# Two ways to bring modulated rows back by token, and a later landing time for gathers

## The chip, the cores and the metric

The kernel is one program on one NeuronCore of a Trainium2 chip. Its metric is the device time of the whole program, in microseconds (us). The engines that work side by side are TensorE (PE in the profile, with its weight loads as PEld), VectorE (DVE), ScalarE (ACT), GpSimd (POOL) and SyncE (SP, which here only issues DMA transfers). Each engine takes its own instructions strictly in the order in which the program lists them, and engines meet by semaphores. Operands lie in SBUF (the on-chip memory of 128 partitions), matmul results in PSUM.

## The reference

There are two layers on `x` of shape 4 batches x 1024 tokens x 256 features, all in float32. Each layer has an attention-like part and a mixture of 8 experts, and before each part a layer norm is modulated with rows that depend on the batch alone:

```python
mod = (_silu(L0_c) @ L0_wmod).reshape(L0_c.shape[0], 6, 1, -1)
sa, ca, ga, sb, cb, gb = (mod[:, 0], mod[:, 1], mod[:, 2], ...)
h = _layernorm(x, axis=-1) * (1 + ca) + sa
x = x + ga * _L0_attn_ref(h, L0_attn_queries, L0_attn_combiners)
h = _layernorm(x, axis=-1) * (1 + cb) + sb
x = x + gb * _L0_ffn_ref(h, L0_ffn_W1, L0_ffn_b1, L0_ffn_W2, L0_ffn_b2, L0_ffn_Wr, L0_ffn_br)
```

The first attention is linear: per head it needs the Gram matrix of the modulated rows `h` over the tokens of a batch, some small products with the query and combiner weights, and one product of `h` with the result. The first expert layer takes the two best of 8 experts for every token. The second layer has the same frame, with a chunked gated MLP for attention and plain matrices as experts.

## The kernel before, in words

**Tiles and stages.** A chunk is 128 tokens of one batch; there are 4 batches `b` of 8 chunks. A "half" is four chunks of a batch, named by a key `(1, b, g)` before the attention and `(2, b, g)` before the experts, so there are 16 halves. The first stage (from 0 to 112.48 us of the span, where the first expert matmul `p_h` L1597 starts) does the attention of layer 0 and the routing. The expert stage and the second layer follow.

**What a half goes through.** `normalised` takes statistics on DVE (L1094, L1095, then L1098 adds the epsilon to the variance), a square root on ACT (L1102), a reciprocal with a Newton step on DVE (L1106 to L1113), and the scaling on ACT (`xn<-x_sb`, L1120). `to_features` turns the 128x128 squares on PE (`pm_t`, L1160), and ACT modulates them while it copies them out of PSUM, with `(1 + c)` and the shift as one number per partition (L1165, to `h1T` or `h2T`). `to_tokens` turns the modulated squares back: 8 turns on PE (`pm_b`, L1187) and two ACT copies (L1192) write the modulated rows over `xn`.

**What needs which form.** For `(1, b, g)` the rows by token feed the Gram matrix (`pm_gram`, L1246, 16 products of a batch, each of which is two records in the profile), whose diagonal blocks DVE copies to `gd` (L1256). Then come a product with the combiners on PE (L1278), an ACT copy (L1288), a product with the queries (`pm_m`, L1299) and the gated copy to `md` on DVE (L1311). `first_half` ends there. `second_half` multiplies the rows by feature with `md` (`pm_o`, L1339), adds to `x_sb` on DVE (L1349), normalises again, turns by `to_features`, computes the router's logits (`pm_e` L194, `le` L1382, `pm_l` L1391), lets DVE choose experts (`route`, 12 operations from L420 to L446) and stores the rows by token, `xn` of `(2, b, g)`, in the DRAM table `h_rows`. The expert stage starts with an indirect DMA by POOL that fetches the rows of the first expert's block from that table (L353), so it waits for the last store.

**What sets the order.** `Plan` is a list scheduler that runs when the program is built. Each piece has an engine, an assumed duration, pieces that it follows, buffer slots, a `rank` (the smaller goes first), an earliest time `at`, and a `lag`: a time after its end at which its result is assumed to be there. `Plan.run` goes through assumed time and puts each piece on its engine's list; the lists are fixed from then on. `FIRSTS` and `SECONDS` are the ranks of the batches' `first_half` and `second_half`. On SP the lists hold the loads and stores, in order: after the gate rows (`gates0`, written to DRAM and read back spread over all partitions as `ga0`), `first_weights` loads W1 and W2 of the last expert into both buffers of each, `w1buf[0]`, `w1buf[1]`, `w2buf[0]` and `w2buf[1]`, then `load_wm1` the second layer's modulation weights, and later the stores to `h_rows`. `kept_busy` puts filler matmuls (`pm_busy`, L1033) into assumed gaps of PE. POOL has nothing to do between its set-up and its first gather.

In the second layer `combine` gathers expert results `yg2` with one POOL DMA each, planned with a `lag` of 1.5 us.

Of the kernel before, what the change touches and what calls it, by code (L numbers as in the profile page):

```python
# [19 lines left out]
P = 128  # L20
B, S, D = 4, 1024, 256
NC = S // P
KD = D // P
E = 8
# [3 lines left out]
EPS = 1e-5  # L28
# [7 lines left out]
FIRST = 8  # L36
ROUTER = 64
STRIP = 32
AHEAD = 3
QUAD = 4  # L40
SQ = 32
# [104 lines left out]
def adaln_d2_kernel(  # L146
# [20 lines left out]
    nc = tc.nc  # L167
# [3 lines left out]
    dram = ctx.enter_context(tc.tile_pool(name="dram", bufs=1, space=DRAM))  # L171
# [48 lines left out]
    def load_mod(wmod, queue, between=()):  # L220
# [8 lines left out]
            )  # L229
        return w  # L230

    busy16 = pa.tile([P, 4 * P], F16, name="busy16", bufs=1)
    nc.vector.memset(busy16, 1.0)
    nc.vector.memset(wr_sb, 0.0)
# [130 lines left out]
    class Pairs:  # L365
# [42 lines left out]
        def route(self, scratch, logits, at, k, step=1):  # L408

            cut = slice(at, at + (k - 1) * step + 1, step)  # L410
            one = self.one[:, :, cut, :]
            shape = [P, k, E]

            def t(tag):
                return scratch.tile(shape, F32, tag=f"r{k}_{tag}", name=f"r_{tag}", bufs=2)

            left = logits
            for i in range(2):
                m = self.best[:, i, cut]
                nc.vector.tensor_reduce(m, left, AX.X, ALU.max)  # L420
                hit = t("hit")
                nc.vector.tensor_tensor(
                    hit, left, m.unsqueeze(2).to_broadcast(shape), ALU.is_equal
                )

                nc.vector.tensor_tensor(
                    hit, hit, rank.unsqueeze(1).to_broadcast(shape), ALU.mult
                )
# [7 lines left out]
                nc.vector.tensor_tensor(  # L436
                    one[:, i, :, :], hit, first.unsqueeze(2).to_broadcast(shape), ALU.is_equal
                )
# [7 lines left out]
            nc.vector.tensor_tensor(both, one[:, 0, :, :], one[:, 1, :, :], ALU.add)  # L446

        def turn(self, pool, h):

# [543 lines left out]


    modT = const.tile([P, 4, B, KD], F32, name="modT")
    gates0 = dram.tile([B, 2, D], F32, name="gates0")
    SA, CA, SB, CB = range(4)
    gds, mds = [
        [pa.tile([P, KD, P], F32, name=f"{x}{i}", bufs=1) for i in range(2)]
# [22 lines left out]
    gate_rows = pa.tile([B, 2, D], F32, name="gate_rows", bufs=1)  # L1022

    stores = []
    plan = Plan(p1=3, p2=2, pm=3, xn1=5, h1T=2, xn2=6, h2T=2, t1=1, le=2)
# [44 lines left out]
    def gate_row(i, column, at):  # L1070
# [12 lines left out]
            rank=-0.5,  # L1083
        )

    def normalised(b, cs, key, slot, after, rank, at=0.0):

        n = len(cs)

        def stats(c):  # L1090
            if c == cs[0]:
                tiles["mv", key] = pa.tile([P, n, 2], F32, tag="ln_mv", name="ln_mv", bufs=6)
            st = pa.tile([P, 6], F32, tag="ln_st", name="ln_st", bufs=4)
            nc.vector.bn_stats(st, x_sb[:, c, b, :])  # L1094
            nc.vector.bn_aggr(tiles["mv", key][:, c - cs[0], :], st)  # L1095
            if c == cs[-1]:
                v = tiles["v", key] = pa.tile([P, n], F32, tag="ln_v", name="ln_v", bufs=6)
                nc.vector.tensor_scalar(v, tiles["mv", key][:, :, 1], EPS, None, ALU.add)  # L1098

        def root():  # L1100
            y = tiles["y", key] = pa.tile([P, n], F32, tag="ln_y", name="ln_y", bufs=6)
            nc.scalar.activation(y, tiles["v", key], AF.Sqrt)  # L1102

        def newton():
            mv, v, y = tiles["mv", key], tiles["v", key], tiles["y", key]
            nc.vector.reciprocal(y, y)  # L1106

            t = pa.tile([P, n], F32, tag="ln_t", name="ln_t")
            nc.vector.scalar_tensor_tensor(t, y, -0.5, y, ALU.mult, ALU.mult)
            nc.vector.tensor_tensor(t, t, v, ALU.mult)  # L1110
            nc.vector.scalar_tensor_tensor(y, t, 1.5, y, ALU.add, ALU.mult)
            m = tiles["m", key] = pa.tile([P, n], F32, tag="ln_m", name="ln_m", bufs=6)
            nc.vector.scalar_tensor_tensor(m, mv[:, :, 0], -1.0, y, ALU.mult, ALU.mult)  # L1113

        def scaled(i):
            if i == 0:
                tiles["xn", key] = pa.tile(
                    [P, n, D], F32, tag=slot[0], name=slot[0], bufs=plan.room[slot[0]]
                )
            nc.scalar.activation(  # L1120
                tiles["xn", key][:, i, :],
                x_sb[:, cs[i], b, :],
                AF.Identity,
                bias=tiles["m", key][:, i : i + 1],
                scale=tiles["y", key][:, i : i + 1],
            )

        last = []
        for i, c in enumerate(cs):
            last = [  # L1130
                plan(
                    DVE,
                    0.54 if i < n - 1 else 0.71,
                    lambda c=c: stats(c),
                    after=[*last, *after(c)],
                    rank=rank,
                    at=at,
                )
            ]
# [37 lines left out]
    def to_tokens(key, slot, src, held, after, rank):  # L1177
# [17 lines left out]
            done.append(plan(ACT, 0.6, out_, after=[m], holds=[ps, slot], rank=rank))  # L1195
        return done

    def buffer(key, tag, shape):


        def get():
            if key not in tiles:
                tiles[key] = pa.tile(shape, F32, tag=tag, name=tag, bufs=plan.room[tag])
            return tiles[key]

        return get

    of_batch = {}

    FIRSTS, SECONDS, SPLIT = [0.0, 1.27, 2.12, 2.24], [1.14, 3.78, 2.27, 3.07], 3  # L1210

    def first_half(b, arrival):

# [4 lines left out]
        for g in range(2):  # L1218
            key, slot = (1, b, g), plan.slot("xn1")
            slots.append(slot)  # L1220
            n = normalised(
                b, range(4 * g, 4 * g + 4), key, slot, lambda c: [], rank, arrival[g]
            )
            cs = slice(4 * g, 4 * g + 4)
            f = to_features(
                b,
                g,
                key,
                slot,
                lambda cs=cs: hT()[:, :, cs, :],  # L1230
                held,
                SA,
                CA,
                [*n, mods_a],
                rank,
            )
            whole += to_tokens(key, slot, lambda cs=cs: hT()[:, :, cs, :], held, f, rank)

        ps, gd, md = plan.slot("p1"), gds[b % 2], mds[b % 2]

# [86 lines left out]
    def second_half(b):  # L1327
# [34 lines left out]
        for g in range(2):  # L1362
# [38 lines left out]
            back = to_tokens(key, slot, hT2, held2, f, rank + 0.1)  # L1401
            backs[g] = (back, slot, key)
        for gs in routed:
            k, at = 4 * len(gs), 4 * gs[0] * B + b
# [43 lines left out]

    mods_a = mods_by_feature((SA, CA), (0, 1), 7.5)
    mods_b = mods_by_feature((SB, CB), (3, 4), 12.0)  # L1450
    rows_done = [gate_row(0, 2, 10.0), gate_row(1, 5, 12.0)]

    def gates_out():
        nc.sync.dma_start(gates0, gate_rows)
# [6 lines left out]

    def first_weights():

        for i in range(2):
            nc.sync.dma_start(w1buf[i], W1[(E - 1) * P :, :])
            nc.sync.dma_start(w2buf[i], W2[(E - 1) * P :, :])

    weights0 = plan("SP", 0.5, first_weights, after=[gate_loaded])
    for at in (15.6, 16.2, 16.8, 18.4, 19.0, 19.6, 21.2, 21.8, 23.4, 91.4, 98.9, 99.4):
        kept_busy(0.44, [], 40.0, at)  # L1470
    for b in range(B):
# [24 lines left out]
        tiles["wm1"] = load_mod(wmod1, nc.sync)  # L1496

    loaded = plan("SP", 0.3, load_wm1, after=[weights0])
    def modulation_rows(before, pieces):
        for piece in pieces:  # L1500
            ps = plan.slot("p2")
# [397 lines left out]
    def combine(key, c, kind, y, g, tile_of, bias, gate, after, rank, at=0.0, stage=None):  # L1899

        done = []
        for b in range(B):
# [3 lines left out]
            for i in range(2):  # L1906
# [19 lines left out]

# [1110 lines left out]
```

## Time and profile before

| quantity | us |
|---|---|
| three runs | 1083.72, 1085.78, 1089.45; median 1085.78 |
| the profiled execution, its own time | 1083.91 |
| span of the profiled execution (first to last instruction) | 1082.2 |
| around the span | 1.7 |
| start of the first expert matmul in the span | 112.48 |

All times below come from that one profiled execution, which lies 1.87 us under the median of the three runs. The mean granted clock of TensorE in it is 0.995 of full speed. The profile's first part gives each engine's busy time; its groups give one line's instructions with count, busy time and mean duration; its waits give the time for which an engine stood idle and what ended that; its windows give busy time by stretch of the span. A matmul's duration runs from its issue to its end, and matmuls are pipelined, so a group's busy time divided by its count is what one costs in a row of them.

### The profile page before, as it was taken

Reading aid. Unit: us, or ns where it says so; the run is one execution under the profiler, and the core shown is the slowest. Engines: PE = TensorE matmul, PEld = TensorE weight load, DVE = VectorE, ACT = ScalarE, POOL = GpSimd, SP = SyncE. Lnnn points to the kernel's source line nnn. Section 1 sums busy time; section 2 is a strip of 40 time slices with the busy share of each in tenths; the row PEclk is TensorE's granted clock in tenths of the full one; section 3 lists DMA queues with packets and bytes.
Section 4 is the critical chain, followed back from the end, with each engine's and each line's share of the span. In section 5 each row is a group of like instructions: output and inputs, shape, how many; then the busy total and the mean of one; then the engine's idle time right before and its main releaser. Section 6 shows DMA issues by size and latency. Waiting matters only on the chain.

```text
span 1082.2 us, 18589 instructions
## 1 busy us (share of the span) xinstructions
PE 1044.7 (97%) x6065; PEld 808.6 (75%) x6065; DVE 601.7 (56%) x2323; ACT 411.1 (38%) x1109; POOL 408.6 (38%) x477
## 2 busy tenths in 40 slices
PE   8999999999999999999999999999999999999993
PEld 5796899889989989998999565664657567646751
DVE  7787443221222222221156488879788736698767
ACT  5977333232322232332344333323224424342531
POOL 2000366555545554553454010100106321573645
PEclk9999999999999999999999999999999999999997
DMA  8504434767462634455171221221014312352534
GB/s 282 217 21 119 171 100 139 272 234 240 140 201 85 225 108 162 146 179 181 41 266 44 75 59 59 61 86 43 19 38 132 117 60 81 100 169 76 155 119 148
DMA packets 94253, 139.78 MB, mean 129 GB/s; under 512 B 31009, under 2 KB 69933, under 8 KB 89542
## 3 DMA queue, kind: packets, MB, share of 16 engines
q0 software_dynamic: 30080, 68.89, 20.4%
q1 hardware_dynamic: 62966, 68.04, 19.5%
q10 hardware_dynamic: 1104, 1.58, 0.4%
q8 instruction: 52, 0.85, 0.3%
q14 instruction: 51, 0.42, 0.1%
HBM read 202.22 MB, written 29.17 MB: 214 GB/s over the span
## 4 chain that ended last, share of the span: by engine, by line
PE 80%; DVE 8%; DMA 4%; issue 4%; ACT 3%; POOL 1%; SPq 0%; DVEq 0%; ACTq 0%; POOLq 0%
PE p_h L1597 21%; PE p_y L1621 19%; PE p_u L2417 19%; PE p_f L2465 8%; PE p_e L2725 4%; PE pm_x L2708 1%; PE pm_counts L847 1%; DMA w<-in_W,g_wrow 1%; ACT xn L1120 1%; PE pm_b L1187 1%; DVE ln_st L1094 1%; PE p_yh L1820 1%; ACT h2T L1165 1%; PE p_hh L1804 1%; DVE step L2798 1%
## 5 line engine op out<-in xcount | busy, mean ns | idle before, releaser
L1609 ACT ACTIVATE hid<-p_h,w 128x128 f32<-128x128 f32 x504 | 144.0, 369 | 298.6 <-issue 206.3
L1621 PE MATMUL p_y<-w,hid 128*128 128x256 f32 x1008 | 230.5, 382 | 1.0 <-DMA w<-in_W,g_wrow 1.0
L2417 PE MATMUL p_u<-hT,a 128*128 128x512 f32 x512 | 229.3, 595 | 1.0 <-ACTq L2382 0.9
L1621 PEld LDWEIGHTS p_y<-w,hid 128*128 128x128 f32 x1008 | 186.9, 190 | 25.0 <-DMA w<-in_W,g_wrow 1.2
L2417 PEld LDWEIGHTS p_u<-hT,a 128*128 128x128 f32 x512 | 94.9, 190 | 102.8 <-issue 92.3
L1597 PEld LDWEIGHTS p_h<-xTq,w 128*128 128x128 f32 x1408 | 163.3, 192 | 1.7
L1597 PE MATMUL p_h<-xTq,w 128*128 128x128 f32 x1408 | 164.5, 275 | 0.0
L353 POOL DMA_INDIRECT w<-in_W,g_wrow x124 | 125.7, 1014 | 67.7 <-ACT hid L1609 42.6
L1632 DVE TENSOR_TENSOR y<-p_y,w 128x256 f32<-128x256 f32 x64 | 27.2, 424 | 193.0 <-PE p_y L1621 193.0
L2465 PE MATMUL p_f<-a,hf 128*128 128x256 f32 x512 | 116.9, 380 | 0.0
L914 POOL DMA_INDIRECT y<-y,g_dest x64 | 66.0, 1031 | 132.3 <-DVE y L1632 71.8
L2465 PEld LDWEIGHTS p_f<-a,hf 128*128 128x128 f32 x512 | 95.9, 190 | 18.7 <-issue 6.4
L2513 POOL TENSOR_TENSOR x_sb<-x_sb,step 128x256 f32<-128x256 f32 x32 | 24.3, 758 | 206.9 <-DVE step L2506 164.1
L860 DVE TENSOR_SCALAR_CACHE_REDUCE g_hits<-pm_counts,g_nth 128x128 f16<-128x128 f32 x68 | 23.6, 347 | 89.2 <-PE pm_counts L847 89.0
L1597 PE MATMUL p_h<-xT,w 128*128 128x128 f32 x608 | 71.3, 275 | 0.5 <-DVE g_dest L881 0.5
L1597 PEld LDWEIGHTS p_h<-xT,w 128*128 128x128 f32 x608 | 70.3, 192 | 1.3 <-DVE xT L1554 0.6
L2429 ACT ACTIVATE hf<-p_u,decay 128x512 f32<-128x512 f32 x56 | 38.2, 685 | 73.2 <-PE p_u L2417 69.8
L2725 PE MATMUL p_e<-ew,xT 128*128 x256 | 65.1, 385 | 0.3 <-ACT y L2735 0.3
L353 POOL DMA_INDIRECT xg<-h_rows,g_row x20 | 19.8, 988 | 109.2 <-DVE g_odd L638 95.8
L2076 DVE TENSOR_TENSOR h<-h,mod 128x256 f32<-128x256 f32 x128 | 51.3, 422 | 5.4 <-ACT h L2066 3.4
L2433 DVE SCALAR_TENSOR_TENSOR hf<-p_u,decay,hf 128x512 f32<-128x512 f32 x56 | 41.8, 747 | 21.4 <-PE p_u L2417 10.7
L353 POOL DMA_INDIRECT xg<-ga_rows,ga_row x36 | 34.5, 957 | 45.6 <-DVE ga_row L869 16.3
(419 smaller groups left out, 1376.3 us busy)
## 6 DMA issues: line engine op xcount, KB each, us to landing
yg<-y SPq DMA_DIRECT2D x32, 256.0 KB
xTq<-square SPq DMA_DIRECT2D x176, 32.0 KB
ew<-in_W SPq DMA_DIRECT2D x16, 288.0 KB
ga_y<-y SPq DMA_DIRECT2D x36, 128.0 KB
half<-in_W SPq DMA_DIRECT2D x16, 257.0 KB
x_sb<-in_x SPq DMA_DIRECT2D x8, 512.0 KB
h_rows<-xn SPq DMA_DIRECT2D x8, 512.0 KB
hT<-square SPq DMA_DIRECT2D x128, 32.0 KB
```

The lines of the kernel that those rows point to most:

```text
L353: return nc.gpsimd.indirect_dma_start(out=dst, out_offset=None, in_=table, in_offset=bass.IndirectOffsetOnAxis(ap=index, axis=0), bounds_c ...
L914: nc.gpsimd.indirect_dma_start(out=table if parts == 1 else table.rearrange("r (i d) -> (r i) d", i=parts), out_offset=bass.IndirectOffset ...
L1597: nc.tensor.matmul(p1[:, i, :], lhsT=w1[:, k * H + m * P : k * H + (m + 1) * P], rhs=xT[k], start=(k == 0), stop=(k == KD - 1),)
L1609: nc.scalar.activation(hid[:, m, :], p1[:, i, :], AF.Relu, bias=w1buf[j % 2][:, KD * H + m : KD * H + m + 1],)
L1621: nc.tensor.matmul(p2, lhsT=hid[:, m, :], rhs=w2[:, m * D : (m + 1) * D], start=(m == 0), stop=(m == KH - 1),)
L1632: nc.vector.tensor_tensor(y, p2, w2buf[j % 2][:, KH * D :], ALU.add)
L2076: nc.vector.tensor_tensor(h, h, mods1[(sc, sh)[i]][:, b, :], (ALU.mult, ALU.add)[i])
L2417: nc.tensor.matmul(pu, lhsT=a[:, k, m * P : (m + 1) * P], rhs=made["n1", c, "hT"][:, k, :, :], start=(k == 0), stop=(k == KD - 1),)
L2429: nc.scalar.activation(made[key, m], made[key, m, 0], AF.Silu, scale=decays[c])
L2433: nc.vector.scalar_tensor_tensor(h, made[key, m, 1], decays[c], h, ALU.mult, ALU.mult)
L2465: nc.tensor.matmul(made[key, "p2", b], lhsT=made[key, m][:, b * P : (b + 1) * P], rhs=a1[:, m, :], start=(m == 0), stop=(m == KH - 1),)
L2725: nc.tensor.matmul(made[key, "p2"], lhsT=made[key, "xT"][:, k, :], rhs=ew_flat[:, bass.ds(made[key, "at"] + k * D, D)], start=(k == 0), st ...
```

## The change

1. **Six halves modulated by token on POOL.** For the keys in `ON_POOL`, `rows_modulated` takes the place of `to_tokens`: for each of the four chunks POOL multiplies the rows of `xn` by `(1 + c)` and then adds the shift, in place, 8 operations of 128x256 in a half. They follow `to_features` of that half, since PE's turns read the same tile before. The rows by feature are made as before.
2. **Rows spread over the partitions.** The operands of POOL have to lie in all partitions. Four `plain_row` pieces (two PE products, that is four records, and one small ACT operation each) extend `gate_rows` and `gates0` from 2 to 6 rows, and three loads of 256 KB spread them over the partitions, into `w1buf[1]` and `w2buf[1]`. The loads of weights into these two buffers move to later on SP: behind POOL's last use of the buffer.
3. **Layer norm.** L1098 is dropped: the square root takes the epsilon as its bias from a tile `eps`, and the Newton step's second operation adds it.
4. **`route`.** Six of its operations change from `tensor_tensor` to `scalar_tensor_tensor` with a factor 1.
5. **Ranks.** New `FIRSTS` and `SECONDS`, so the first stage's lists change on every engine.
6. **Gathers of the second layer.** The `lag` of `combine`'s gathers goes from 1.5 to 2.5 us.

```diff
+ON_POOL = [(1, 2, 0), (1, 2, 1), (1, 3, 0), (1, 3, 1), (2, 0, 0), (2, 0, 1)]
...
-                nc.vector.tensor_tensor(
-                    hit, left, m.unsqueeze(2).to_broadcast(shape), ALU.is_equal
-                )
...
+                nc.vector.scalar_tensor_tensor(
+                    hit, left, 1.0, m.unsqueeze(2).to_broadcast(shape), ALU.mult, ALU.is_equal
+                )
...
-    gates0 = dram.tile([B, 2, D], F32, name="gates0")
+    gates0 = dram.tile([B, 6, D], F32, name="gates0")
...
+    spread = {
+        k: buf[:, : 2 * B * D].rearrange("p (b i d) -> p b i d", b=B, i=2)
+        for k, buf in ((2, w2buf[1]), (1, w1buf[1]))
+    }
...
+    def plain_row(i, column, plus, at):
+        ps = plan.slot("p2")
+        def mm():
+            tiles["gate", i] = mod_rows(sT0, wm0, column * D, D)
+        def out_():
+            if plus:
+                nc.scalar.activation(
+                    gate_rows[:, i, :], tiles["gate", i], AF.Identity, bias=ones[:B, :1]
+                )
+            else:
+                nc.scalar.copy(gate_rows[:, i, :], tiles["gate", i])
...
-            if c == cs[-1]:
-                v = tiles["v", key] = pa.tile([P, n], F32, tag="ln_v", name="ln_v", bufs=6)
-                nc.vector.tensor_scalar(v, tiles["mv", key][:, :, 1], EPS, None, ALU.add)
...
-            nc.scalar.activation(y, tiles["v", key], AF.Sqrt)
+            nc.scalar.activation(y, tiles["mv", key][:, :, 1], AF.Sqrt, bias=eps)
...
-            nc.vector.tensor_tensor(t, t, v, ALU.mult)
+            nc.vector.scalar_tensor_tensor(t, mv[:, :, 1], EPS, t, ALU.add, ALU.mult)
...
+    def rows_modulated(b, key, slot, after, rank):
+        done = []
+        for i in range(4):
+            def scale(i=i):
+                t = tiles["xn", key][:, i, :]
+                nc.gpsimd.tensor_tensor(t, t, spread[key[0]][:, b, 1, :], ALU.mult)
+            def shift(i=i):
+                t = tiles["xn", key][:, i, :]
+                nc.gpsimd.tensor_tensor(t, t, spread[key[0]][:, b, 0, :], ALU.add)
+            d = plan(POOL, 0.75, scale, after=[*after, spread_in[key[0], b]], holds=[slot], rank=rank)
+            done.append(plan(POOL, 0.75, shift, after=[d], holds=[slot], rank=rank))
+        spread_used[key[0]].extend(done)
+        return done
...
-    FIRSTS, SECONDS, SPLIT = [0.0, 1.27, 2.12, 2.24], [1.14, 3.78, 2.27, 3.07], 3
+    FIRSTS, SECONDS, SPLIT = [0, 0.41, 1.0, 1.46], [1.4, 4.85, 4.69, 0.06], 3
...
-            whole += to_tokens(key, slot, lambda cs=cs: hT()[:, :, cs, :], held, f, rank)
+            if key in ON_POOL:
+                whole += rows_modulated(b, key, slot, f, rank)
+            else:
+                whole += to_tokens(key, slot, lambda cs=cs: hT()[:, :, cs, :], held, f, rank)
...
-        for i in range(2):
-            nc.sync.dma_start(w1buf[i], W1[(E - 1) * P :, :])
-            nc.sync.dma_start(w2buf[i], W2[(E - 1) * P :, :])
...
+        nc.sync.dma_start(w1buf[0], W1[(E - 1) * P :, :])
+        nc.sync.dma_start(w2buf[0], W2[(E - 1) * P :, :])
...
+    for k in (1, 2):
+        for b in (0, 2, 3, 1):
+            if any((k, b, g) in ON_POOL for g in range(2)):
+                spread_in[k, b] = plan(
+                    "SP", 0.1, lambda k=k, b=b: rows_in(k, b), after=[q], rank=-0.7, lag=3.5
+                )
...
+    for k, buf, w in ((1, w1buf[1], W1), (2, w2buf[1], W2)):
+        plan(
+            "SP",
+            0.3,
+            lambda buf=buf, w=w: nc.sync.dma_start(buf, w[(E - 1) * P :, :]),
+            after=[*spread_used[k], weights0],
+            rank=3.6,
+            lag=6.0,
+        )
...
-                            lag=1.5,
+                            lag=2.5,
```

More of the change, by code (lines that the diff above doesn't have):

```diff
@@ L230, in load_mod @@
         return w
+    eps = pa.tile([P, 1], F32, name="eps", bufs=1)
+    nc.vector.memset(eps, EPS)
     busy16 = pa.tile([P, 4 * P], F16, name="busy16", bufs=1)
@@ L421, in route @@
                 hit = t("hit")
-                nc.vector.tensor_tensor(
-                    hit, left, m.unsqueeze(2).to_broadcast(shape), ALU.is_equal
-                )
-                nc.vector.tensor_tensor(
-                    hit, hit, rank.unsqueeze(1).to_broadcast(shape), ALU.mult
+                nc.vector.scalar_tensor_tensor(
+                    hit, left, 1.0, m.unsqueeze(2).to_broadcast(shape), ALU.mult, ALU.is_equal
+                )
+                nc.vector.scalar_tensor_tensor(
+                    hit, hit, 1.0, rank.unsqueeze(1).to_broadcast(shape), ALU.mult, ALU.mult
                 )
@@ L435, in route @@
                 nc.vector.tensor_reduce(first, hit, AX.X, ALU.max)
-                nc.vector.tensor_tensor(
-                    one[:, i, :, :], hit, first.unsqueeze(2).to_broadcast(shape), ALU.is_equal
+                nc.vector.scalar_tensor_tensor(
+                    one[:, i, :, :],
+                    hit,
+                    1.0,
+                    first.unsqueeze(2).to_broadcast(shape),
+                    ALU.mult,
+                    ALU.is_equal,
                 )
@@ L445, in route @@
             both = self.both[:, at + 1 : at + (k - 1) * step + 2 : step, :]
-            nc.vector.tensor_tensor(both, one[:, 0, :, :], one[:, 1, :, :], ALU.add)
+            nc.vector.scalar_tensor_tensor(
+                both, one[:, 0, :, :], 1.0, one[:, 1, :, :], ALU.mult, ALU.add
+            )
         def turn(self, pool, h):
@@ L1021, in adaln_d2_kernel @@
     sT1 = silu_of(1, c1)
-    gate_rows = pa.tile([B, 2, D], F32, name="gate_rows", bufs=1)
+    gate_rows = pa.tile([B, 6, D], F32, name="gate_rows", bufs=1)
+    spread = {
+        k: buf[:, : 2 * B * D].rearrange("p (b i d) -> p b i d", b=B, i=2)
+        for k, buf in ((2, w2buf[1]), (1, w1buf[1]))
+    }
     stores = []
@@ L1084, in gate_row @@
         )
+    def plain_row(i, column, plus, at):
[9 more added lines that the diff above has]
+                nc.scalar.copy(gate_rows[:, i, :], tiles["gate", i])
+        m = plan(PE, 0.9, mm, holds=[ps], at=at, rank=-0.5)
+        return plan(ACT, 0.45, out_, after=[m], holds=[ps], rank=-0.5)
     def normalised(b, cs, key, slot, after, rank, at=0.0):
@@ L1095, in stats @@
             nc.vector.bn_aggr(tiles["mv", key][:, c - cs[0], :], st)
-            if c == cs[-1]:
-                v = tiles["v", key] = pa.tile([P, n], F32, tag="ln_v", name="ln_v", bufs=6)
-                nc.vector.tensor_scalar(v, tiles["mv", key][:, :, 1], EPS, None, ALU.add)
         def root():
             y = tiles["y", key] = pa.tile([P, n], F32, tag="ln_y", name="ln_y", bufs=6)
-            nc.scalar.activation(y, tiles["v", key], AF.Sqrt)
+            nc.scalar.activation(y, tiles["mv", key][:, :, 1], AF.Sqrt, bias=eps)
         def newton():
-            mv, v, y = tiles["mv", key], tiles["v", key], tiles["y", key]
+            mv, y = tiles["mv", key], tiles["y", key]
             nc.vector.reciprocal(y, y)
@@ L1132, in normalised @@
                     DVE,
-                    0.54 if i < n - 1 else 0.71,
+                    0.54,
                     lambda c=c: stats(c),
@@ L1206, in buffer @@
         return get
-    of_batch = {}
-    FIRSTS, SECONDS, SPLIT = [0.0, 1.27, 2.12, 2.24], [1.14, 3.78, 2.27, 3.07], 3
+    of_batch, spread_in, spread_used = {}, {}, {1: [], 2: []}
+    FIRSTS, SECONDS, SPLIT = [0, 0.41, 1.0, 1.46], [1.4, 4.85, 4.69, 0.06], 3
     def first_half(b, arrival):
@@ L1400, in second_half @@
                 of_batch["routed"] = ready[g][0]
-            back = to_tokens(key, slot, hT2, held2, f, rank + 0.1)
+            if key in ON_POOL:
+                back = rows_modulated(b, key, slot, f, rank + 0.1)
+            else:
+                back = to_tokens(key, slot, hT2, held2, f, rank + 0.1)
             backs[g] = (back, slot, key)
@@ L1450, in adaln_d2_kernel @@
     mods_b = mods_by_feature((SB, CB), (3, 4), 12.0)
-    rows_done = [gate_row(0, 2, 10.0), gate_row(1, 5, 12.0)]
+    rows_done = [
+        gate_row(0, 2, 10.0),
+        gate_row(1, 5, 12.0),
+        plain_row(4, 0, False, 10.0),
+        plain_row(5, 1, True, 10.0),
+        plain_row(2, 3, False, 12.0),
+        plain_row(3, 4, True, 12.0),
+    ]
     def gates_out():
@@ L1462, in first_weights, with rows_in @@
     def first_weights():
-        for i in range(2):
-            nc.sync.dma_start(w1buf[i], W1[(E - 1) * P :, :])
-            nc.sync.dma_start(w2buf[i], W2[(E - 1) * P :, :])
-    weights0 = plan("SP", 0.5, first_weights, after=[gate_loaded])
+        nc.sync.dma_start(w1buf[0], W1[(E - 1) * P :, :])
+        nc.sync.dma_start(w2buf[0], W2[(E - 1) * P :, :])
+    def rows_in(k, b):
+        cut = slice(4, 6) if k == 1 else slice(2, 4)
+        nc.sync.dma_start(spread[k][:, b, :, :], gates0[b, cut, :].partition_broadcast(P))
+    for k in (1, 2):
[4 more added lines that the diff above has]
+                )
+    weights0 = plan("SP", 0.5, first_weights, after=[gate_loaded, *spread_in.values()])
     for at in (15.6, 16.2, 16.8, 18.4, 19.0, 19.6, 21.2, 21.8, 23.4, 91.4, 98.9, 99.4):
```

## The prediction, made before the changed kernel ran

> **What bounds the kernel now.** The change lies in the first stage and in one assumption of the second layer, so I read the page's first part, then the stage by windows, then what each engine waited for there.
>
> The page's busy totals: the columns give busy us, share of the span and instructions.
>
> ```profile
> PE 1044.7 (97%) x6065; PEld 808.6 (75%) x6065; DVE 601.7 (56%) x2323; ACT 411.1 (38%) x1109; POOL 408.6 (38%) x477
> ```
>
> By these alone PE bounds everything. The windows of the first stage (busy us of PE, PEld, DVE, ACT, POOL, then clock and DMA) show more than one tight engine:
>
> ```profile
> 20.00:46.00 26.00, 23.67 (x197) 21.05 (x196) 23.62 (x104) 23.28 (x49) 0.00 (x0) 1.00 0.68 256
> 46.00:86.00 40.00, 39.03 (x391) 34.59 (x390) 30.64 (x116) 32.74 (x67) 0.00 (x0) 1.00 0.14 41
> 86.00:103.20 17.20, 15.83 (x155) 10.50 (x155) 12.75 (x62) 15.04 (x31) 0.00 (x0) 1.00 0.42 117
> ```
>
> POOL does nothing there. PE is full from 46 to 86. What DVE waited for from 8.4 to 103.2 is 10.4 us in all; the longest entries (us, times, longest):
>
> ```profile
> DVE ln_y L1106 <- ACT ln_y L1102: 3.6, 4, 2.7
> DVE g_best L420 <- PE pm_l L1391: 3.2, 3, 1.8
> DVE x_sb L1349 <- PE pm_o L1339: 1.4, 2, 1.2
> ```
>
> So DVE is occupied for 94.8 - 10.4 = 84.4 us of this stretch, start-up times between instructions included. PE's windows hold 88.6 us there, 8.7 of them fillers (`pm_busy`, L1033). The two are about level: relieving PE alone helps only until DVE is full.
>
> The end of the stage in the chain that ended last:
>
> ```profile
> 102.89 0.19 DVE g_both L446
> ...
> 109.28 2.77 DMA xg<-h_rows,g_row
> 112.09 0.39 PE pm_x L1549
> 112.48 0.56 PE p_h L1597 x5
> ```
>
> The last route ends on DVE at 103.1, and 9.4 us later the experts start; what matters is when DVE, and the stores of the rows, finish.
>
> **The change part by part.** The groups for the removed work in the stage, and for POOL's operation where the kernel already has it, in the second layer (durations in ns, min/median/max):
>
> ```profile
> L1187 PE MATMUL pm_b<-ident,h2T 128*128 128x128 f32 x64 | 9.4, 280 | 0.4 <-ACT h2T L1165 0.4
> L1187 PE MATMUL pm_b<-ident,h1T 128*128 128x128 f32 x64 | 9.2, 277 | 1.7 <-ACT h1T L1165 1.5
> ```
>
> ```profile
> L1192 ACT COPY xn<-pm_b 128x512 f32<-128x512 f32 x32 | 17.5, 591 | 0.8 <-PE pm_b L1187 0.7
> ```
>
> ```profile
> L2513 POOL TENSOR_TENSOR x_sb<-x_sb,step x32: 722/729/901, 637.0 to 1009.8; 128x256 f32<-128x256 f32 x32
> ```
>
> *PE.* 18.6 us for 128 turns is 0.145 each; 6 halves x 8 turns = 48 turns leave, -7.0 us, nearly all from the full stretch. The four row pieces add 4 x 1.05 = 4.2 us (L325: 8 records, 2.1 us, for two such rows), at 10 to 23 us, where fillers stood. They cost nothing as long as they take filler time; if they hold up the first Gram matrix (24.0), up to 2. I take 0.
>
> *ACT.* 12 of 32 copies leave, 12 x 0.547 = -6.6 us; the rows add 2 x 0.36 + 2 x 0.46 = 1.6 (L350, L348, the same forms at 107 to 112). ACT has 15.6 us of waits in the stretch, so this gives room, no time by itself.
>
> *DVE.* L1098 leaves 16 times at about 0.2 start to start: -3.2 us. The Newton step's changed operation stays at 161 to 162 ns by the rows beside it; `route`'s six keep their duration (L441, already of the new form, 207 against 211 to 213). One memset is added at the start, under the first loads, nothing.
>
> *POOL.* 48 operations at 0.76 (the mean of L2513) are 36.4 us on an engine that was idle. By the lists it starts behind the turns of `(1,2,0)`, which I put at 46 us by the instructions that precede them, then does `(1,2,*)`, `(1,3,*)`, `(2,0,*)` in this order. Alone it ends at 82.4. The Gram matrices of batches 2 and 3 wait for 16 and 32 of these: 46 + 12.2 = 58 and 70, where in the profile of before their diagonals were copied at 60.1 and 73.2. So POOL is just in time, with no reserve of its own.
>
> *What POOL does to DVE.* Idle POOL becomes a neighbour that works for 36 us beside DVE. The trace has such overlaps in the second layer. Here a DVE operation on two SBUF operands (424 ns elsewhere) started under a POOL operation:
>
> ```profile
> 641.64 0.90 POOL L2513 TENSOR_TENSOR x_sb<-x_sb,step 128x256 f32<-128x256 f32 x1 [2.79 <-DVE step L2506]
> 641.99 0.83 DVE L1958 TENSOR_TENSOR yg<-yg,gb 128x256 f32<-128x256 f32 x1
> ```
>
> It took 0.83 and ended 0.28 after POOL's, and POOL's took 0.90 where 0.73 is its median: each waits for the other. A small `scalar_tensor_tensor` behaves alike (L2606: median 196, longest 384, under a POOL operation), so the new form in `route` and in the Newton step gives no protection. Statistics (417 to 419) and operations with one operand in PSUM (L2487, 483 against 482 to 484) are not touched. In POOL's stretch the lists of DVE hold about 6 Newton steps with four two-operand instructions each and one route with six: 30 instructions. The five small ones hit in the trace (L2604, L2606 twice, L817 twice) lost 0.21, 0.19, 0.19, 0.30 and 0.47, mean 0.27; some start while POOL waits. I take 0.25, 30 x 0.25 = +7.5 us. Low end: a third are hit, +2. High end: a Newton step's instructions follow one another, and each meets the next POOL operation and loses all of 0.73 but its own 0.17: 30 x 0.56 = +16.8. POOL itself loses up to 30 x 0.17 = 5.1 and then ends at 87.5.
>
> The Trainium skill ("SBUF — State Buffer", "Who interferes with whom") says that a DVE instruction with two SBUF inputs contends with a GpSimd instruction that reads SBUF, and that whoever issues second blocks fully. Its kinds of instruction agree with the rows above; an estimate from full blocking at a random moment is half of 0.73, so 0.36 each and 11 us in all, and with that the sum below would end at +4.8. It speaks against this change. I keep the rows' mean, since POOL also pauses.
>
> *Waits of DVE after.* From the lists: the start on the first load 1.2 as now; roots on ACT 2 of 3.6, since ACT is relieved; the last `pm_l` 1.8 as now; new is 2.4 for batch 2, where `md` follows `gd` with nothing between (0.9 + 0.57 + 0.66 for L1278, L1288, L1299, and hand-overs). Together 7.4 instead of 10.4.
>
> *SP.* Three loads of 256 KB come in among the first weights, and 2.2 MB leave that burst; nothing reads either soon. The second W1 stands behind 32 POOL operations, the second W2 behind 48, and SP keeps its order: the stores of five halves (512 KB each, some 1.5 us) and the routes' small stores are queued behind. From 87.5 these are 1.15 MB and 2.6 MB, 11 us at 340 GB/s, done at 99, before the last route (103.1): nothing, as long as POOL ends before about 91; then one for one. The weights are read at about 121 and 129 us, nothing.
>
> *The gathers' lag.* PE's, POOL's and SP's lists do not change after the first stage; only some DVE and ACT instructions swap places, near 940 to 975 and in the last 40 us, which gathers of 1.27 us each pace. Nothing, within 2 us either way.
>
> *Sum.* DVE: 84.4 - 3.2 + 7.5 + 7.4 = 96.1 against 94.8: +1.3 on the profiled 1083.9, so 1085.2. The median of the runs stood 1.9 above that execution; I name 1086.
>
> **The rivals.**
>
> *A: faster, POOL and DVE hardly meet.* For it: POOL waits for `pm_t` of each half, and Newton steps are short. With +2 and waits of 5: 84.4 - 3.2 + 2 + 5 = 88.2, -6.6, and PE, 7 us lighter in its full stretch, can follow. Against it: the 32 operations of batches 2 and 3 leave POOL few pauses. Time 1078 to 1080.
>
> *B: slower, the Newton steps lose a POOL operation each time.* The place is 46 to 88, the price 0.56 for each of 30: 84.4 - 3.2 + 16.8 + 7.4 = 105.4, +10.6, so 1094 to 1096. It decides (over +5.4) from 0.39 lost per instruction, 11.6 us in all. For it: they come in fours, back to back. Against: no hit instruction but one of the trace lost that much.
>
> *C: nothing arrives at all.* The end of the stage hangs on the last stores, whose rows of batches 1 to 3 are still turned back by PE and copied by ACT. If PE's fillers and the final chain keep their times, the stage ends where it did: 1084 to 1086. For it: the last window has ACT at 15.0 of 17.2, and no work leaves it there.
>
> **How the numbers follow.** About 0.5%, 5.4 us, is what a measurement of this kernel tells from no change. The forecast gets 0.36 and C 0.06, both within it; A 0.27, B 0.31. Range: low from A with its waits at the short end, 1078; high from B, 1096; it leaves out more extreme waits, some 0.2. The likeliest case alone, with losses of 0.15 to 0.38 per instruction, spans 1082 to 1090.
>
> **What would show it.** Right: DVE's small two-operand instructions between 46 and 88 at 0.3 to 0.5 instead of 0.16 and 0.2; POOL's at 0.73 to 0.90, done by 82 to 88; DVE waits near 7 us; the first `p_h` at 113 to 115. Wrong for A: those instructions at 0.16 and `p_h` near 106. Wrong for B: losses above 0.4 and `p_h` past 118. The prediction is also wrong if PE idles for POOL's rows before the Gram matrices of batches 2 and 3 while nothing else stands ahead on its list: each us there is lost directly, and a lower granted clock would show it, which is 1.00 in every window now.

## The result, and the profile after

The changed kernel takes 1090.96 us (median of 8 runs, 1090.44 to 1091.56) against 1086.2 us for the kernel before in the same comparison (8 runs, 1083.72 to 1089.45): a ratio of 1.0043, 95% interval 1.0030 to 1.0056. It is 4.8 us slower. The profiled execution took 1090.44 us (span 1088.7), 6.5 us more than the profiled one of before, which lay at the lower end of its runs.

Nearly all of it arises in the first stage. Its landmarks in the two traces, in us (read from the timelines of DVE, POOL and PE):

| landmark | before | after | difference |
|---|---|---|---|
| Gram matrix of batch 0 starts | 24.0 | 25.5 | +1.5 |
| Gram matrix of batch 2 starts | 56.3 | 57.7 | +1.4 |
| diagonal `gd` of batch 2 starts | 60.1 | 66.5 | +6.4 |
| last route of the first stage ends | 103.1 | 107.8 | +4.8 |
| first fetch by POOL | 107.9 | 113.7 | +5.9 |
| first expert matmul `p_h` | 112.3 | 118.1 | +5.8 |
| an expert matmul `p_h` in the middle of the expert stage | 293.3 | 300.0 | +6.7 |
| last matmul | 1066.8 | 1073.1 | +6.3 |

The timeline has the first `p_h` of before at 112.32; the 112.48 given ahead of the prediction is where the chain that ended last comes to these matmuls, not where they start.

The same three windows as before (busy us of PE, PEld, DVE, ACT, POOL, then clock, DMA share, GB/s):

```profile
20.00:46.00 26.00, 24.83 (x215) 21.80 (x212) 22.49 (x96) 24.06 (x50) 0.41 (x1) 1.00 0.62 205
46.00:86.00 40.00, 32.73 (x305) 28.36 (x303) 30.43 (x91) 26.22 (x51) 33.58 (x48) 0.96 0.23 67
86.00:103.20 17.20, 13.98 (x141) 10.80 (x140) 14.37 (x63) 13.99 (x29) 0.00 (x0) 0.90 0.47 133
```

From 46 to 86 PE went from 39.0 to 32.7 busy and ACT from 32.7 to 26.2: the work did leave. POOL is busy for 33.6, as planned. What nothing before had shown is the column of the clock: 0.96 and 0.90 instead of 1.00.

What PE waited for from 45 to 84 (us, times, longest):

```profile
PE pm_t L1327 <- DVE gd L1305: 6.0, 2, 4.8
PE pm_o L1388 <- DVE x_sb L1398: 1.0, 1, 1.0
```

PE stood still for 4.8 us at one place, 62.3 to 67.2: ahead of the product with the combiners of batch 2, for the diagonal that DVE copies. The Gram matrix itself was done at 61.45. In the kernel before, DVE stood ready when the Gram matrix of batch 2 was done, and copied at once:

```profile
60.10 0.59 DVE L1256 COPY gd<-pm_gram 64x128 f32<-64x128 f32 x2 [0.30 <-PE pm_gram L1246]
```

Now DVE was late, and a stretch of its timeline beside POOL's says why (start, us, engine, line):

```profile
48.58 0.74 POOL L1233 TENSOR_TENSOR xn<-xn,w 128x256 f32<-128x256 f32 x1
48.58 0.75 DVE L1137 SCALAR_TENSOR_TENSOR ln_t<-ln_y 128x4 f32<-128x4 f32 x1
49.37 0.16 DVE L1138 SCALAR_TENSOR_TENSOR ln_t<-ln_mv,ln_t 128x4 f32<-128x4 f32 x1
49.39 0.75 POOL L1237 TENSOR_TENSOR xn<-xn,w 128x256 f32<-128x256 f32 x1
49.57 0.59 DVE L1139 SCALAR_TENSOR_TENSOR ln_y<-ln_t,ln_y 128x4 f32<-128x4 f32 x1
50.09 0.73 POOL L1233 TENSOR_TENSOR xn<-xn,w 128x256 f32<-128x256 f32 x1
50.19 0.65 DVE L1141 SCALAR_TENSOR_TENSOR ln_m<-ln_mv,ln_y 128x4 f32<-128x4 f32 x1
```

Here a Newton instruction of 0.16 us takes 0.59 to 0.75 when POOL's operation is already running, and ends with it; the one that starts in the gap between two of POOL's (49.37) takes 0.16. POOL is hardly held up: its 48 operations took 0.728 on average and ended at 81.5. In POOL's stretch DVE has 22 such instructions, four Newton steps of four and one route of six; 16 of them lost more than 0.04 us, 6.57 us together, counted against 0.162 for a Newton instruction and 0.225 for a route's. Of this, 5.16 us lie ahead of the diagonal of batch 2, which starts 5.1 us after its Gram matrix was done.

### The profile page after: what moved, and what is told of

Same layout as the page of the kernel before. It is cut to its first block, busy times and chain, and to the rows that moved or that the text cites. A ratio compares the mean times of both kernels' runs of the same rounds, so it can differ in the third digit from the quotient of the medians.

```text
span 1088.7 us, 18556 instructions
## 1 busy us (share of the span) xinstructions
PE 1044.6 (96%) x6033; PEld 807.7 (74%) x6033; DVE 605.0 (56%) x2308; ACT 407.7 (37%) x1101; POOL 441.3 (41%) x525
## 5 line engine op out<-in xcount | busy, mean ns | idle before, releaser
L2803 PEld LDWEIGHTS p_e<-ew,xT 128*128 128x128 f32 x256 | 44.9, 191 | 9.1 <-issue 2.9
```

Source lines behind the costliest of these rows:

```text
L2803: nc.tensor.matmul(made[key, "p2"], lhsT=made[key, "xT"][:, k, :], rhs=ew_flat[:, bass.ds(made[key, "at"] + k * D, D)], start=(k == 0), st ...
```

## The experiments

The runs e1 to e4 and e9 to e12 were made where the kernel before itself took 1111 and 1117 us. Up to the last route the first stage is the same there (103.0 in e11, which has that of before, against 103.1; 107.6 in e4, which has the changed one, against 107.8), but in e11 the first `p_h` comes 0.5 later, so landmarks after the route agree only to about that. Times are compared as ratios to the kernel before run beside them, and the first stage by its landmarks: end of the last route and start of the first `p_h`, 107.8 and 118.1 in the changed kernel, 103.1 and 112.3 before.

**The lag put back (e4).**

```diff
-                            lag=2.5,
+                            lag=1.5,
```

> The changed kernel with the gathers' assumed landing back at 1.5 us. If the lag does what it says, the second layer loses 0.3 to 1.5 us again. If it does nothing, the time stays within 0.5 us of the changed kernel (1091). The first stage is the same in both, p_h at 118.

Ratio 1.0060 (1.0035 to 1.0086); route end 107.6, `p_h` 118.2. Since the first stage is the changed kernel's, this is above all a second profile of it: PE's stall (4.8 us) comes again, and DVE loses 6.2 us in 15 of 22 instructions. The times of this chip can't be set against the changed kernel's 1091, so the lag is not decided by this run.

**The lag alone, in the kernel before (e11).**

```diff
-                            lag=1.5,
+                            lag=2.5,
```

> The kernel before with the gathers' lag at 2.5 alone. By the prediction nothing, within 2 us either way; if the lag is what raised the end of the changed kernel, 1 to 3 us slower; the first stage is that of before, p_h at 112.3 to 112.7.

Ratio 1.0033 (1.0002 to 1.0064), `p_h` 112.8. On this chip, where runs of one kernel lie 13 to 14 us apart, the lag is a small loss if any, with an interval that only just leaves out zero; in the profiles of the changed kernel the second layer gives back 0.5 us between its first and last matmul. How much the lag does on the chip of the main result stays open; it is not what makes the 5.8 us of the first stage.

**POOL emptied (e2).**

```diff
-ON_POOL = [(1, 2, 0), (1, 2, 1), (1, 3, 0), (1, 3, 1), (2, 0, 0), (2, 0, 1)]
+ON_POOL = []
```

> The changed kernel with an empty list for POOL: PE and ACT turn all 16 halves back, everything else (new ranks, layer norm, route, lag, the added rows, the moved weights) as changed. Theory 'POOL costs': without it the layer norm's 3 us and the new order are left, p_h starts at 108 to 112, and the kernel is 0 to 4 us faster than before. Rival 'the new order costs': the ranks fit only with POOL, p_h starts at 114 to 119 and the kernel is as slow as the changed one or slower.

Ratio 1.0081 (1.0051 to 1.0112), route end 108.8, `p_h` 117.8. The rival held: the new ranks without POOL are as slow as the changed kernel. So this run doesn't give the price of POOL; the lists that the planner makes from these ranks need POOL's relief.

**The old ranks with POOL (e6).**

```diff
-    FIRSTS, SECONDS, SPLIT = [0, 0.41, 1.0, 1.46], [1.4, 4.85, 4.69, 0.06], 3
+    FIRSTS, SECONDS, SPLIT = [0.0, 1.27, 2.12, 2.24], [1.14, 3.78, 2.27, 3.07], 3
```

> The changed kernel with the ranks of before. Theory 'contention, whatever the order': p_h at 116 to 120, DVE loses 5 to 8 us to POOL again. Rival 'the new order is what costs': with the old order the POOL version reaches p_h at 109 to 112.

Ratio 1.0100 (1.0076 to 1.0124), route end 113.6, `p_h` 122.1, past both expectations. DVE lost 5.1 us beside POOL, and waited 5.1 at one time for a Gram matrix: the one of batch 2 started at 70.2. The ranks of either kernel fit only its own way of modulating.

**Layer norm and route alone (e7).** The kernel before, with the change's `normalised` and `route` and the `eps` tile. The ranks are those of before, but the planner is told of the shorter statistics and orders its lists anew:

```diff
-                nc.vector.tensor_scalar(v, tiles["mv", key][:, :, 1], EPS, None, ALU.add)
...
-            nc.scalar.activation(y, tiles["v", key], AF.Sqrt)
+            nc.scalar.activation(y, tiles["mv", key][:, :, 1], AF.Sqrt, bias=eps)
...
-            nc.vector.tensor_tensor(t, t, v, ALU.mult)
+            nc.vector.scalar_tensor_tensor(t, mv[:, :, 1], EPS, t, ALU.add, ALU.mult)
```

> The kernel before with the change's layer norm and route alone. By the step of the prediction DVE loses 3.2 us of work: if DVE sets the pace, p_h starts at 109 to 111 instead of 112.4; if PE does, 111.5 to 113, and the time is within 1 us of before.

Ratio 1.0002 (0.9988 to 1.0015), route end 104.3, `p_h` 112.7. DVE has 16 operations less, about 3 us, and nothing comes out: the time is the same within 1.6 us, and the last route ends 1.2 later. Its waits for PE grew instead: 5.5 us for `pm_o` where it had 1.4. So less work on DVE alone did not bring the end of this stage forward; as the lists differ too, the run doesn't say what the same lists would have given.

**POOL that only writes (e3).** Each of POOL's operations becomes three memsets; the rows of the six halves stay unmodulated and one column of them is zero. There is one execution, so only its landmarks are used.

```diff
-                nc.gpsimd.tensor_tensor(t, t, spread[key[0]][:, b, 1, :], ALU.mult)
+                nc.gpsimd.memset(t[:, :1], 0.0)
+                nc.gpsimd.memset(spread[key[0]][:, b, 1, :], 0.0)
+                nc.gpsimd.memset(spread[key[0]][:, b, 0, :], 0.0)
```

> The changed kernel, where POOL's 48 operations are replaced by memsets of about the same length (0.7 us in all for each) at the same places and behind the same waits: they write the spread rows and one column of xn and read nothing, so the six halves go on unmodulated but for that column, set to 0; the routing of the other rows stays nearly the same. Theory 'contention': DVE's instructions on two SBUF operands fall back from 0.4 to 0.75 to 0.16 and 0.23 us, 6.6 us of DVE come back, PE's stall of 4.8 us before batch 2's combiners shrinks to under 2, the clock stays at 1.00 there, and p_h starts at 110 to 113.5. Rival 'order and POOL's chain': the Gram matrices wait for POOL all the same, p_h starts at 116 to 118.

Route end 100.0, `p_h` 110.9, the clock 1.00 in every window. DVE's instructions from 40 to 90:

```profile
L1137 DVE SCALAR_TENSOR_TENSOR ln_t<-ln_y 128x4 f32<-128x4 f32 x9 | 1.5, 163 | 0.3
L1139 DVE SCALAR_TENSOR_TENSOR ln_y<-ln_t,ln_y 128x4 f32<-128x4 f32 x9 | 1.5, 162 | 0.3
L429 DVE SCALAR_TENSOR_TENSOR r_hit<-r_hit,rank 128x64 f32<-128x64 f32 x4 | 0.9, 225 | 0.1
```

They are back at 162 and 225 ns with POOL working beside them, and the diagonal of batch 2 comes at 61.7 instead of 66.5. One thing is not equal: memsets follow each other faster, and POOL was done at about 72 instead of 81.5. The Gram matrix of batch 2 started at 57.2, only 0.5 earlier, so the diagonal's 4.8 us are not POOL's earlier end; what the rest owes to it this run doesn't part.

**DVE's operands in PSUM (e5).** POOL does its real work again. DVE reads at most one operand from SBUF in the Newton steps of five halves, two instructions more for each, and in all of the instructions of batch 0's route but the last:

```diff
+            if key in IN_PSUM:
+                pt = psum(ps_2, [P, 2, n], "pm_n")
+                r, t = pt[:, 0, :], pt[:, 1, :]
+                s = pa.tile([P, n], F32, tag="ln_s", name="ln_s")
+                nc.vector.reciprocal(s, y)
+                nc.vector.reciprocal(r, y)
...
-            nc.vector.scalar_tensor_tensor(t, y, -0.5, y, ALU.mult, ALU.mult)
+            nc.vector.scalar_tensor_tensor(t, r, -0.5, s, ALU.mult, ALU.mult)
...
+            def t(tag, i=0):
+                if spare is not None:
+                    q = 1 + i if tag == "hit" else 3
+                    return spare[:, :, q * E : (q + 1) * E]
```

Here `IN_PSUM` holds the halves (2,0,1), (2,1,0), (2,1,1), (2,2,0), (2,2,1), and `spare` is the tile of `pm_l`, of which the logits use 8 of every 32 columns.

> The changed kernel, its lists and POOL's work as they are, but DVE's instructions that ran beside POOL read at most one operand from SBUF: for five halves the reciprocal is also written to PSUM and the Newton step goes on there (two instructions more, about 0.4 us a half), and the route of batch 0 keeps its masks in spare columns of its PSUM tile (its last instruction still reads two from SBUF). Theory 'contention': these instructions fall from 0.4 to 0.75 to about 0.2, DVE gains 4 to 5 us net, PE's stall before batch 2's combiners falls from 4.8 to 1 to 2.5, and the first p_h starts at 112 to 115 instead of 118.1. Rival 'reads were not the matter' (the memsets were merely quicker than the products): durations stay, p_h at 117 to 119.

The lists of PE, DVE and ACT in the first stage are those of the changed kernel. Ratio 0.9987 (0.9977 to 0.9998): 1083.47 us against 1084.29. Route end 101.1, `p_h` 111.2, the diagonal of batch 2 at 62.7, the clock 1.00 throughout, and POOL at work from 46.3 to 82.3 as in the changed kernel. DVE from 46 to 83:

```profile
L1148 DVE SCALAR_TENSOR_TENSOR pm_n<-pm_n,ln_s 128x4 f32<-128x4 f32 x5 | 0.9, 170 | 0.2
L1149 DVE SCALAR_TENSOR_TENSOR pm_n<-ln_mv,pm_n 128x4 f32<-128x4 f32 x5 | 0.8, 166 | 0.2
L1156 DVE SCALAR_TENSOR_TENSOR ln_m<-ln_mv,pm_n 128x4 f32<-128x4 f32 x5 | 0.8, 158 | 0.2
L433 DVE SCALAR_TENSOR_TENSOR pm_l<-pm_l,rank 128x64 f32<-128x64 f32 x2 | 0.5, 233 | 0.1
```

PE's waits for the diagonals fell from 6.0 us in two places (4.8 of it for batch 2) to 0.7 in one:

```profile
PE pm_t L1342 <- DVE gd L1320: 0.7, 1, 0.7
PE pm_o L1403 <- DVE ln_m L1156: 0.7, 1, 0.7
```

With the engines' order as the change makes it and POOL's operations untouched, the second operand from SBUF is worth 6.9 us at `p_h` (118.1 to 111.2, one profile each). The version beats both kernels, the one before by 0.1% (0.02% to 0.23%).

**The planner told of the waits (e8).**

```diff
-        d = plan(DVE, 0.9, newton, after=[r], rank=rank - 0.2)
+        d = plan(DVE, 2.2 if key in SLOWED else 0.9, newton, after=[r], rank=rank - 0.2)
...
-                0.24 * 13 + 0.16 * 4 if k == NC else 0.22 * 13,
+                4.9 if b == 0 else 0.24 * 13 + 0.16 * 4 if k == NC else 0.22 * 13,
```

`SLOWED` holds the same five halves.

> The changed kernel, but the planner is given the durations that DVE showed beside POOL: 2.2 us for five halves' Newton steps, 4.9 for batch 0's route. In the lists one Newton step then goes behind the diagonal of batch 2. Theory 'contention acts through what stands ahead of the diagonal': the diagonal comes about 2 us sooner, PE's stall falls to about 3, p_h at 115 to 117. If only DVE's sum counts, p_h stays at 117.5 to 118.5.

Ratio 0.9997 (0.9984 to 1.0010), route end 105.1, `p_h` 113.6. DVE loses as much beside POOL as in the changed kernel, 7.1 us in 18 of 23 instructions, but the diagonal comes at 62.3, directly behind the route:

```profile
61.62 0.77 DVE L455 SCALAR_TENSOR_TENSOR g_both<-g_one 128x64 f16<-128x64 f16 x1
62.31 0.58 DVE L1306 COPY gd<-pm_gram 64x128 f32<-64x128 f32 x2
62.92 0.18 DVE L1135 RECIPROCAL ln_y<-ln_y 128x4 f32<-128x4 f32 x1
63.14 0.67 DVE L1138 SCALAR_TENSOR_TENSOR ln_t<-ln_y 128x4 f32<-128x4 f32 x1
```

In the changed kernel one more pair of statistics and a whole Newton step, slowed by POOL, stood between the two:

```profile
62.93 0.77 DVE L454 SCALAR_TENSOR_TENSOR g_both<-g_one 128x64 f16<-128x64 f16 x1
63.62 0.41 DVE L1125 BATCH_NORM_STATS2 ln_st<-x_sb 128x6 f32<-128x256 f32 x1
...
65.15 0.65 DVE L1138 SCALAR_TENSOR_TENSOR ln_t<-ln_mv,ln_t 128x4 f32<-128x4 f32 x1
...
66.52 0.58 DVE L1305 COPY gd<-pm_gram 64x128 f32<-64x128 f32 x2
```

The clock fell here too, to 0.50 for 6.8 us from 64.5 on. Statistics are planned elsewhere now too, so not all of the 4.6 us at `p_h` is that one swap; but the sum that DVE loses is the same, and the loss in time is gone. (The first `p_h` came sooner than the 115 to 117 that the expectation had for this.)

**PE kept busy in its stalls (e1, e10).** Fillers go ahead of the product with the combiners of batch 2 (20 matmuls), and ahead of a turn back of half (2,1,1) (8 matmuls), the second one of the half in e1, the first in e10:

```diff
+            if b == 2:
+                for _ in range(20):
+                    nc.tensor.matmul(
+                        p1.rearrange("p a b -> p (a b)"), lhsT=busy16[:, :P], rhs=busy16[:, : 4 * P], start=True, stop=True
+                    )
...
+                if key == (2, 1, 1) and i == 0:
+                    for _ in range(8):
```

> The changed kernel, with filler matmuls on PE in the two places where it stood still before its clock was halved: 20 (about 4.3 us at full clock) ahead of the product with the combiners of batch 2, 8 (1.7 us) ahead of the second turn back of half (2,1,1). Theory 'clock': the two halved stretches of 3.4 us each cost 1.5 to 3 us of the 4.8 on the path; the granted clock is 1.00 from 60 to 100, the first p_h starts at 115 to 116.5 instead of 118.1, and the time falls by 1.5 to 3 us against the changed kernel. Theory 'contention alone': PE had slack there, the clock is 1.00 and p_h still starts at 117.5 to 118.5.

Ratio 1.0106 (1.0067 to 1.0144), `p_h` 120.1. The first fillers did their work: the product with the combiners takes 1.13 us instead of 2.08. The second ones were misplaced. Their PSUM tile was still held by ACT, so they came after the stall, at half clock, and added 3.39 us ahead of the turn. So e10:

> The changed kernel with fillers on PE in both stalls, the second now ahead of the first turn back of half (2,1,1), where its PSUM tile is free. Theory 'clock': granted clock 1.00 from 60 to 100, p_h at 115 to 117 instead of 118.1, 1 to 3 us gained. Rival 'the halved stretches had slack': 0.7 us at most, from the first; p_h at 117.2 to 118.5.

Ratio 1.0053 (1.0028 to 1.0078), route end 106.5, `p_h` 117.0. The same two windows in e10,

```profile
60.00:72.00 12.00, 11.00 (x92) 7.25 (x91) 7.19 (x21) 6.12 (x13) 11.37 (x17) 1.00 0.13 15
92.00:100.00 8.00, 6.97 (x69) 4.38 (x67) 6.96 (x34) 7.71 (x17) 0.00 (x0) 1.00 0.44 106
```

and in the changed kernel:

```profile
60.00:72.00 12.00, 7.16 (x67) 5.61 (x67) 6.80 (x20) 5.77 (x12) 11.37 (x17) 0.86 0.16 30
92.00:100.00 8.00, 5.91 (x57) 4.53 (x57) 5.99 (x29) 6.85 (x15) 0.00 (x0) 0.79 0.37 105
```

The clock is whole again, DVE still loses 6.4 us beside POOL, and `p_h` gains 1.15 us (1.2 against e4, and 1.1 to 1.4 at the last route). That is about the clock's share of the 5.8, from one profile. The whole time shows no gain: 1.0053 here, 1.0043 and 1.0060 for the changed first stage without fillers.

**Both remedies together (e9, e12).** The PSUM operands of e5, with the costs of e8 in e9, and with costs that fit the PSUM forms in e12:

```diff
-        d = plan(DVE, 0.9, newton, after=[r], rank=rank - 0.2)
+        d = plan(DVE, 1.4 if key in IN_PSUM else 0.9, newton, after=[r], rank=rank - 0.2)
...
-                0.24 * 13 + 0.16 * 4 if k == NC else 0.22 * 13,
+                3.3 if b == 0 else 0.24 * 13 + 0.16 * 4 if k == NC else 0.22 * 13,
```

> The masks and Newton steps in PSUM as in the run that did that, with the planner's costs of the run that gave it the longer durations. If the two gains (about 5 us each against the changed kernel) were of different kinds, both come: p_h at 108 to 110, the time 3 to 5 us under before. If they are the same gain twice, a shorter way to batch 2's diagonal, p_h stays at 110.5 to 112 and the time within 2 us of before.

> As the first of these, with costs for the planner that fit the PSUM forms (1.4 for a Newton step, 3.3 for the route). Lists in which the costs are right should be as good or better: p_h at 108 to 110.5. If the order hardly matters once DVE is undisturbed, p_h at 110.5 to 112.

Ratios 1.0003 (0.9976 to 1.0029) and 1.0023 (0.9997 to 1.0049); `p_h` 113.4 and 113.5, later than either expectation for both. The gains don't add. In e12 the last route ends at 99.6, the earliest of all kernels, 8 us before the changed kernel's, and yet the first fetch is at 108.7. What PE waited for from 84 to 118:

```profile
PE pm_x L1643 <- DMA xg<-h_rows,g_row: 4.7, 1, 4.7
PE pm_t L1203 <- ACT h2T L1208: 2.1, 1, 2.1
```

The second W2 left at 82.8 and six of the eight stores of 512 KB after it; the DMA share from 86 to 103 is 1.14 (0.47 in the changed kernel), and the last rows land at about 106. So the transfers behind POOL's last operation are what `p_h` waits for in this run, on this slower chip. In e5 the second W2 left at the same time (82.7), and the first fetch came 5.7 us after the last route, not 9.1; whether the transfers limit that chip too wasn't tried.

## Why the prediction was right, and where its steps failed

The forecast was no change to be told apart, 1086 us with 1078 to 1096. The measured 1090.96 lies inside, and 0.43% is under the bound of 0.5%, though eight runs of each kernel do tell these 4.8 us from nothing; it lies just outside the 1082 to 1090 of the likeliest case alone. Of the signs that the prediction named for itself, DVE's slower instructions and POOL's end came about as said. DVE's waits (12.5 us, not near 7) and the first `p_h` (118.1, not 113 to 115) did not, and a `p_h` past 118 was rival B's sign. The last route ended 99.4 us after 8.4, where the sum had 96.1. So the time lies in the range partly by luck: the cause was named, contention between POOL and DVE, but the step from it to the time failed. Point by point:

- *PE and ACT.* Right: 6.3 us of PE and 6.5 of ACT left the stretch from 46 to 86 (7.0 and 6.6 in the sum). The four added rows were taken at 0 with up to 2 as bound. The first Gram matrix comes 1.5 later in the changed kernel, 1.2 later in e6, which has the rows and the ranks of before, and 0.5 later in e7, which has no rows. So they put it off by about 1; whether any of that reaches the end no run shows.
- *POOL.* Right: start 45.6 (46), rows for the Gram matrix of batch 2 done at 57.65, just in time for its start at 57.7 (58), end 81.5 (82.4 alone). That POOL would lose up to 5.1 us was wrong; 0.728 per operation is its undisturbed duration, and DVE alone pays.
- *What POOL does to DVE.* The sum was right by two errors: 30 instructions at 0.25 made 7.5, the trace has 22 that lose 6.57, or 0.30 each and 0.41 for each one hit. Three of the five rows behind the 0.25 (L2604 and L817 twice) are `tensor_scalar` instructions with one tensor operand, so they were no measure of instructions on two. Rival B's condition, 0.39 for every one of 30, was not met in the sum, but its picture of a Newton step that meets one POOL operation after the other is what the timeline shows. The estimate from the Trainium skill ("SBUF — State Buffer", "Who interferes with whom"), 0.36 for each of 30, is as far above the measured 0.30 as 0.25 is below. That the sum would have ended with it at +4.8, the difference then measured, is luck, since DVE's sum is not what set the end. The page's rule that a second SBUF operand is what contends, and only with a GpSimd instruction that reads, agrees with both runs that took one side away: e3 (163 ns beside memsets) and e5 (158 to 170 ns beside the products).
- *The sum over DVE.* This step failed. It took DVE's occupied time plus its waits as the end of the stage. e7 takes 16 operations from DVE and the time stays (1.0002), in lists that changed with it; e8 leaves DVE's loss at 7.1 us and the loss in time is gone (0.9997). What counted was which of DVE's instructions stood ahead of the diagonal of batch 2. The prediction put the price of contention into DVE's total and a wait of PE for that diagonal at nothing; the trace has a wait of 4.8 us there.
- *Waits of DVE after.* Mis-sized for that reason: 7.4 in the sum, 12.5 in the trace up to 108, with 3.9 for batch 2's `pm_m` and 1.4 for the `pm_o` that follows, both after PE's stall of 4.8. Occupied, DVE was 86.9 us (107.8 - 8.4 - 12.5) where the prediction had 88.7.
- *The clock.* The prediction named PE's idling for late rows with a lower clock as what would make it wrong. PE idled for DVE instead, and the clock did fall: about 1 us at `p_h` by e10, and nothing that the whole time shows.
- *SP.* Taken at nothing. From the last route to the first fetch it is now 5.9 us instead of 4.8; why the last stores land 1.1 later wasn't tried apart, but in e12, on its slower chip, these transfers carry the end.
- *The lag.* Nothing by the prediction; not decided (e4, e11). Another 0.8 us, lost between 118 and 155 us in the expert stage, is not explained either.
- *The rivals.* A fell: POOL never waits between its first operation and its last, and DVE's instructions lost 0.41 on average when hit. Its outcome came only when the contention was taken away by hand (e5), and was then 1.1 us at `p_h`, not 6. C fell with the moved landmarks.

## What to carry to other kernels

When an idle engine gets work beside VectorE, count the VectorE instructions with two SBUF operands in that stretch, and ask of each what stands behind it on its list: here 6.6 us lost ahead of another engine's next product came with 4.8 us more in time (the changed kernel), and 7.1 us lost in another order with none (e8). Moving one operand to PSUM frees such an instruction at the price of a copy or a second write. When a list scheduler fixed the order, its durations have to include the neighbour's effect: giving it the slowed durations alone made up for the loss here.

## What the runs showed of the hardware that was not expected

POOL and DVE do not share alike: in a row of POOL operations of 0.73 us DVE's short instructions were held up and POOL kept its pace (0.748 us from start to start on average, 35.9 us for 48). POOL's records leave a gap of about 0.07 us between a chunk's multiply and its add (49.32 to 49.39 above) and none between the add and the next multiply (50.14 and 50.09). DVE got one short instruction through in such a gap and waited out both operations that follow, so 11 of the 16 Newton instructions were hit.

In the changed kernel the clock fell twice for 3.4 us. By windows of 1 us of the changed kernel it was 0.50 from 67 to 70, after the stall of 4.8 us:

```profile
66.00:67.00 1.00, 0.00 (x0) 0.00 (x0) 0.96 (x3) 0.36 (x1) 1.00 (x2) 0.98 0.00 0
67.00:68.00 1.00, 0.84 (x2) 0.75 (x3) 0.11 (x1) 1.00 (x3) 0.92 (x2) 0.50 0.00 0
```

It fell again from 94.3 to 97.7, after a stall of only 2.1 us (92.0 to 94.1) with 1.6 us of turns (`pm_t`, `pm_l`, `pm_b`) before it and no product from 90.4 to 95.9. The Trainium skill ("TensorE: Matmul & The Clock Gate", "What's actually happening") gives about 3.4 us of idling for the halved clock, which the first fall agrees with; in its Part 4 it says that turns don't count as busy in the same way. The runs don't need that for the second fall. By the trace's record of the clock, the falls and rises in the changed kernel's first stage lie whole multiples of 3.41 us apart (66.96, 70.38, 94.27, 97.68). Here are the 3.41 us ahead of each fall, and those ahead of the fall in e8:

```profile
63.55:66.96 3.41, 0.00 (x0) 0.00 (x0) 2.80 (x10) 0.62 (x2) 3.25 (x6) 1.00 0.00 0
90.86:94.27 3.41, 1.32 (x13) 1.08 (x12) 3.10 (x15) 3.39 (x8) 0.00 (x0) 1.00 0.46 159
61.13:64.54 3.41, 1.32 (x6) 0.70 (x5) 3.19 (x9) 0.31 (x1) 3.18 (x5) 1.00 0.00 0
```

PE was busy for 39% of the second stretch, with turns, and for the same 39% of the third, with products alone. So a fall does not need PE to be idle throughout. Nor does the stall alone decide: in e4, with the same first stage, the same stall of 2.1 us (92.8 to 94.9) left the clock at 1.00, and its one fall, after the stall of 4.8 us, lasted 6.8 us instead of 3.4. There the stall lies across two of the steps of 3.41 us (90.24 to 93.65 and 93.65 to 97.06, with PE busy for 2.57 and 2.15 us). That its place against these steps decides, and at what share, no run tried apart.
